# Queries and keys of three attention rows: one dense product each, spread to row groups through DRAM

## The chip, the cores and the metric

The kernel runs on one core of one Trainium2 chip. A core has five engines with their own instruction streams: PE (TensorE, matrix products), DVE (VectorE), ACT (ScalarE), POOL (GpSimd) and SP (SyncE), which here mostly issues DMAs. Each stream runs strictly in its order, and streams wait for each other through semaphores. In the profile, PEld is the loading of weights into PE, and PEq and SPq are the queues of PE and SP. The metric is the device time of one execution in microseconds. Three runs of the kernel before took 1353.03, 1360.2 and 1360.58 us, median 1360.2.

## The reference

Two layers, each of them attention plus a mixture of experts, both reading the same normalised input:

```
x  = [4, 512, 128]                         # 4 rows of 512 tokens, 128 features
xn = layernorm(x);  x = x + band_attention(xn) + gated_experts(xn)    # layer 0: 16 heads, window 64; 16 experts
xn = layernorm(x);  x = x + full_attention(xn) + relu_experts(xn)     # layer 1
```

What the change touches is the full attention of layer 1:

```
q, k, v = split(xn @ w_qkv)                # w_qkv [128, 384]; 16 heads of 8 features
attn    = softmax(q k^T / sqrt(128))       # per row and head, 512 x 512
out     = (attn v, heads side by side) @ w_out
```

All of it is in float32. The full attention is computed for every row, and the ReLU experts of a row need the same normalised row.

## The kernel before

Data is kept with features on the 128 partitions and tokens along the free dimension: `xT` holds the normalised rows of layer 1, 512 columns for each row. The kernel has two stages. In the first, which lasts to about 933 us, layer 0 is computed for the four rows, woven with the band attention of the row before (`band_values`) and with the first ReLU experts of layer 1 (`relu_experts`). In the second, from line 749 on, `full_attention` is woven with three things that are left over: the band values of the last row, the experts of row 2 and then the experts of row 3.

**The steps.** A head has 8 features, so four heads (a "group") are put into the four bands of 32 partitions of the PE array: head h of the group has partitions 32h to 32h+7. There are 4 rows with 4 groups each, so 16 groups, and in a group 4 blocks of 128 tokens, and in a block two pairs of heads. A pair of heads makes one score tile of 128 x 2 x 512 in PSUM. Each pair is computed twice: once ("m") keys by queries, where DVE takes the maximum over all keys (L952), and later ("x"), with that maximum worked into the product, where ACT takes the exponential (L959). The m pairs run twelve pairs ahead of the x pairs (`AHEAD`). One step of the loop normally has one m pair and one x pair, and with the first and last steps there are 128 steps. The four products of a step use four different bands of the array and are tied together by hand (`in_order`), and the first of a step waits until the maximum and the exponential of the step before have freed their PSUM tiles. With high priority, so ahead of all else, come the scores, the maxima, the exponentials and the weighting of values by a finished block (`weigh`, L852).

**Work between the scores.** Everything else is hung on steps by `at(t, ...)`: `queries` and `keys` a few steps ahead of a group's first m pair, `values` of a row, `with_maxima` after the last m pair of a group, `normalise` (two operations on DVE after a transposition), and at the end of a row `turned` and `project_out` (L882). They all take their PSUM tile from one buffer, `abank`. Between them stand the products of the ReLU experts (L388 in, L454 out), which are held to the pace of the steps by dependencies that only fix an order, and the band values: L321 transposes, L322 copies, L327 stores to DRAM (`by_s`), L339 loads back skewed (`wb`), L353 and L357 multiply. The framework's scheduler puts all instructions into one fixed order for each engine when the kernel is built.

**Queries and keys.** For the bands, the weights are spread out once with zeros: `wqk` has 32 columns for each head, of which 8 are filled. A group's queries are then one product of 128 x 128 by 128 x 512 (L823), of which only 4 x 8 of 128 output partitions hold anything, copied from PSUM by ACT (L827); the keys are another such product (L832), copied with a bias (L836) that puts a 1 into partition 32h+8, against which the negative maximum from the first pass is multiplied. So a row takes 8 such products, 4 groups by 2. `with_maxima` adds the transposed maxima to the queries (L843). `ex`, the exponentials of one block for four heads, has three buffers of 8 KB on each partition (`ep`).

**Other lines used later.** POOL sets up `wqk` (L765), the padded values `vaug` (L775, L776) and the maxima `nmax` (L777) at the start of the stage, and adds up the experts (L459). SP issues, in this order, what is ready: expert weights (L440, L442), routing rows (L444), band transfers (L312 `f`, L327, L339), and finished rows (L887).

Of the kernel before, what the change touches and what calls it, by code (L numbers as in the profile page):

```python
# [22 lines left out]
FP = mybir.dt.float32  # L23
# [5 lines left out]
P = 128  # L29
B, T, C = 4, 512, 128  # L30
# [67 lines left out]
def two_layers(ctx: ExitStack, tc: tile.TileContext, w: dict, consts: bass.AP, out: bass.AP):  # L98
    nc = tc.nc
# [5 lines left out]
    dram = ctx.enter_context(tc.tile_pool(name="dram", bufs=1, space=bass.MemoryType.DRAM))  # L105
# [19 lines left out]
    def c_(name):  # L125
        return cst[:, offs[name][0]:offs[name][1]]
# [160 lines left out]
    xT = keep.tile([C, B * T], FP, name="xT")  # L287
# [461 lines left out]
    ctx1 = ctx.enter_context(ExitStack())  # L749
    work = ctx1.enter_context(tc.tile_pool(name="work", bufs=2))  # L750
    one = ctx1.enter_context(tc.tile_pool(name="one", bufs=1))
    ep = ctx1.enter_context(tc.tile_pool(name="ep", bufs=3))
    ps_q = ctx1.enter_context(tc.tile_pool(name="ps_q", bufs=1, space=PSUM))
    ps_a = ctx1.enter_context(tc.tile_pool(name="ps_a", bufs=1, space=PSUM))

    def abank():
        return ps_a.tile([P, T], FP, tag="a", name="abank")

    w_qkv = one.tile([C, 3 * C], FP, name="w_qkv")
# [6 lines left out]
    for s in range(2):  # L766
        nc.vector.tensor_copy(
            wqk[:, s, :, :, 0:8].rearrange("c g h e -> c (g h) e"),
            w_qkv[:, s * C:(s + 1) * C].rearrange("c (h e) -> c h e", e=8),
        )  # L770

    vaug = [one.tile([P, TPB, H, 32], FP, name=f"vaug{i}") for i in range(2)]
    nmax = [one.tile([P, TPB, 4, 32], FP, name=f"nmax{i}") for i in range(2)]
# [8 lines left out]
    def full_attention():  # L782
# [6 lines left out]
        outs, q, k, qa, av, ex = {}, {}, {}, {}, {}, {}  # L789
# [18 lines left out]
        def values(b):  # L808
            pv = abank()
            for i in range(TPB):  # L810
                nc.tensor.matmul(  # L811
                    pv[:, i * P:(i + 1) * P], xT[:, b * T + i * P:b * T + (i + 1) * P],
                    w_qkv[:, 2 * C:3 * C], start=True, stop=True,
                )
            nc.vector.tensor_copy(
                vaug[b % 2][:, :, :, 0:8], pv.rearrange("p (t h e) -> p t h e", t=TPB, e=8)
            )
            outs[b] = work.tile([P, TPB, C], FP, tag="o1", name="o1")

        def queries(n):  # L820
            b, g = groups[n]
            pq = abank()
            nc.tensor.matmul(  # L823
                pq, wqk[:, 0, g].rearrange("c h e -> c (h e)"), xT[:, b * T:(b + 1) * T], start=True, stop=True
            )
            q[n] = work.tile([P, T], FP, tag="q", name="q")
            nc.scalar.copy(q[n], pq)  # L827
# [63 lines left out]
        def at(t, f, *args):  # L891
            todo.setdefault(t, []).append((f, args))
# [8 lines left out]
        for j in range(AHEAD, len(pairs)):  # L901
            x_step[j - AHEAD] = m_step[j] = len(steps)
            n, i, two = pairs[j - AHEAD]
# [4 lines left out]

        for n, (b, g) in enumerate(groups):
            t = m_step[8 * n]  # L910
            at(t - 5 if n > 1 else t - 3, queries, n)
            at(t - 3 if n > 1 else t - 2, keys, n)
            if g == 0:
                at(t + 1, values, b)
            at(m_step[8 * n + 7] + 1, with_maxima, n)
            for i in range(TPB):
                at(x_step[8 * n + 2 * i + 1] + 1, weigh, n, i)
            t = x_step[8 * n + 7]
            at(t + 3, normalise, n)
            if g == 3:  # L920
                at(t + 5, turned, b)
                at(t + 6, project_out, b)
# [43 lines left out]
    x_out = out.rearrange("b (t p) c -> p b t c", p=P)  # L966
    weave(
        (full_attention(), 106),
        (after(woven((band_values(B - 1, ready[B - 1][1]), 23), (experts[B - 2], 42)), relu_experts(B - 1)), 22 + 42 + 79 + 4),
    )  # L970
# [35 lines left out]
```

## Time and profile before

| | us |
|---|---|
| median of three runs | 1360.2 |
| the profiled execution, its own time | 1354.64 |
| its span, first to last instruction | 1352.8 |
| PE busy | 1165.9 |
| ACT busy | 1018.8 |
| DVE busy | 1007.9 |
| POOL busy | 87.3 |
| mean granted PE clock | 0.941 |

The busy times are of the whole execution and mix two stages with different limits; only the stage from about 933 us on has instructions of the lines that the diff touches. In the rows of groups of instructions, the first number is the time in which the engine was busy with the group, then the mean of one instruction in ns, then the idle time of the engine just ahead of them. PE appears with two records for each float32 product. In rows of the timeline the start and the length are in us, and the bracket at the end is the time in which the engine stood idle before, with the instruction that ended it.

### The profile page before, as it was taken

How to read it: one execution, taken by the hardware profiler on the slowest of the kernel's cores; microseconds unless marked ns; L12 is line 12 of the kernel's file. 1: busy time of each engine (PE TensorE's matmuls, PEld its weight loads, DVE VectorE, ACT ScalarE, POOL GpSimd, SP SyncE). 2: the span in 40 equal slices, each digit the busy share in tenths (PEclk: the TensorE clock that was granted, in tenths of full speed). 3: DMA queues.
4: the chain of work that ended last, by engine and by line, in shares of the span. 5: the costliest groups of instructions: out<-in, count | busy, mean ns of one | idle time of the engine just before them, and what ended most of it. 6: DMA issues, size and time to landing. Idle time of an engine off the chain costs nothing. (4 is left out here: it accounts for less than half of the span.)

```text
span 1352.8 us, 17415 instructions
## 1 busy us (share of the span) xinstructions
PE 1165.9 (86%) x6763; PEld 448.1 (33%) x6763; DVE 1007.9 (75%) x1085; ACT 1018.8 (75%) x1159; POOL 87.3 (6%) x68
## 2 busy tenths in 40 slices
PE   5676976677899879988987998897999999999997
PEld 2122322133434323334332343343333334333332
DVE  4999998999878899997779999843544445544441
ACT  4899997989888899999879999863454445555454
POOL 2000000000001021100100300002000000000000
PEclk9798988888999979998998999996999989999999
DMA  8121211446223434721244463223333210010100
GB/s 273 49 75 50 77 53 67 129 101 158 70 59 81 164 94 123 188 65 61 80 154 99 125 156 100 73 67 133 94 94 78 54 41 25 27 36 24 47 24 8
DMA packets 168524, 117.61 MB, mean 87 GB/s; under 512 B 66621, under 2 KB 149274, under 8 KB 166906
## 3 DMA queue, kind: packets, MB, share of 16 engines
q1 hardware_dynamic: 166970, 109.77, 29.6%
q0 software_dynamic: 1184, 6.29, 1.2%
q8 instruction: 54, 0.88, 0.3%
q10 hardware_dynamic: 288, 0.43, 0.1%
q14 instruction: 28, 0.23, 0.1%
HBM read 89.00 MB, written 27.46 MB: 86 GB/s over the span
## 5 line engine op out<-in xcount | busy, mean ns | idle before, releaser
L572 DVE TENSOR_TENSOR z<-proj 128x2044 f32<-128x2044 f32 (+31 forms) x256 | 553.6, 2185 | 22.6 <-PE lbank L586 13.5
L586 PE MATMUL lbank<-z,place 128*32 128x504 f32 (+18 forms) x2048 | 294.5, 649 | 105.3 <-ACT z L578 61.1
L952 DVE TENSOR_REDUCE nmax<-score 128x2 f32<-128x1024 f32 x128 | 156.3, 1225 | 194.1 <-PE score L935 193.7
L578 ACT ACTIVATE z<-z,posb 128x1024 f32<-128x1024 f32 (+31 forms) x256 | 266.7, 1097 | 8.1 <-DVE z L572 6.3
L574 ACT ACTIVATE z<-z,brep 128x2048 f32<-128x2048 f32 (+31 forms) x128 | 241.6, 1904 | 8.1 <-DVE z L572 7.0
L959 ACT ACTIVATE ex<-score 128x1024 f32<-128x1024 f32 x128 | 130.3, 1023 | 138.9 <-PE score L935 138.9
L935 PE MATMUL score<-k,q 32*128 32x512 f32 x512 | 142.6, 668 | 6.5 <-DVE nmax L952 4.0
L388 PE MATMUL bank<-xT,ew 128*128 128x512 f32 x256 | 137.0, 627 | 6.9 <-DVE e L628 5.7
L935 PE MATMUL score<-qa,k 32*128 32x512 f32 x512 | 139.5, 647 | 2.0 <-ACT ex L959 1.4
L459 POOL TENSOR_TENSOR total<-total,part 128x512 f32<-128x512 f32 x32 | 73.0, 2280 | 1044.1 <-DVE part L458 1018.2
L396 ACT ACTIVATE h<-bank,cols 128x512 f32<-128x512 f32 x144 | 97.8, 685 | 49.5 <-PE bank L388 48.9
L454 PE MATMUL bank<-h,ew 128*128 128x512 f32 x256 | 132.2, 614 | 2.5 <-ACT h L396 2.5
L586 PEld LDWEIGHTS lbank<-z,place 128*32 128x32 f32 x2048 | 44.3, 113 | 263.7 <-ACT z L578 128.7
L675 PEld LDWEIGHTS accbank<-wT,lin 128*128 128x128 f32 x512 | 71.3, 204 | 64.5 <-issue 38.3
L675 PE MATMUL accbank<-wT,lin 128*128 128x128 f32 x512 | 82.7, 300 | 9.0 <-DVE lin L673 8.9
L686 PE MATMUL gbank<-tT,wT 128*128 128x512 f32 x128 | 71.7, 642 | 19.1 <-DMA wT<-wT_all 18.3
L852 PE MATMUL accbank<-ex,vaug 128*32 128x512 f32 x512 | 70.6, 617 | 0.2 <-ACT ex L959 0.2
L693 PE MATMUL gbank<-tT,wT 128*128 128x512 f32 x128 | 67.4, 608 | 0.0
L689 ACT ACTIVATE glu<-gbank,gbt 128x512 f32<-128x512 f32 x64 | 43.8, 685 | 29.2 <-PE gbank L686 28.6
L454 PEld LDWEIGHTS bank<-h,ew 128*128 128x128 f32 x256 | 44.2, 193 | 59.6 <-issue 47.6
L935 PEld LDWEIGHTS score<-k,q 32*128 32x128 f32 x512 | 38.8, 190 | 75.2 <-ACT ex L959 31.3
L388 PEld LDWEIGHTS bank<-xT,ew 128*128 128x128 f32 x256 | 41.8, 193 | 66.2 <-issue 44.8
(188 smaller groups left out, 1192.3 us busy)
## 6 DMA issues: line engine op xcount, KB each, us to landing
r<-route SPq DMA_DIRECT2D x96, 256.0 KB, 3.4
ew<-in_L_ffn_W SPq DMA_DIRECT2D x64, 256.0 KB, 2.8
wb<-by_s SPq DMA_DIRECT2D x32, 512.0 KB, 5.5
wT<-wT_all SPq DMA_DIRECT2D x48, 192.0 KB, 2.4
by_t<-e SPq DMA_DIRECT2D x8, 1024.0 KB, 4.8
f<-by_t SPq DMA_DIRECT2D x128, 64.0 KB, 3.0
by_s<-g SPq DMA_DIRECT2D x16, 512.0 KB, 4.2
wb<-by_s SPq DMA_DIRECT2D x24, 256.0 KB, 3.0
```

The costliest lines, as they stand in the source:

```text
L388: mm = nc.tensor.matmul(ph, wt[:, c * P:(c + 1) * P], xT[:, b * T:(b + 1) * T], start=True, stop=True)
L396: nc.scalar.activation(h, ph, AF.Relu, bias=bias[:, c:c + 1])
L454: nc.tensor.matmul(py, old[1][:, c, :], old[0][c], start=(c == 0), stop=(c == 3))
L459: nc.gpsimd.tensor_tensor(total, total, part, ALU.add)
L572: nc.vector.tensor_tensor(z[:, :, :, 0:n], seen, own, ALU.subtract)
L574: nc.scalar.activation(z[:, :, :, 0:n], z[:, :, :, 0:n], AF.Gelu, bias=b_dmg)
L578: last = nc.scalar.activation(z[:, dq, :, 0:n], z[:, dq, :, 0:n], AF.Gelu, bias=posb[:, j:j + 1])
L586: mm = nc.tensor.matmul(ps[q:q + 32, t0:T], place[:, kind, 3 - dd:35 - dd], z[:, dq, hg, 0:n], start=(dd == 0), stop=(dd == 3),)
L675: nc.tensor.matmul(ya[:, i * P:(i + 1) * P], lin[:, i * P:(i + 1) * P], wT[:, 2, :], start=False, stop=(e == E0 - 1 and i == TPB - 1),)
L935: mm = nc.tensor.matmul(ps[:, h - two, :], own[r, i * P:(i + 1) * P], seen[r, :], start=True, stop=True)
L952: freed.append(nc.vector.tensor_reduce(nmax[n % 2][:, i, two:two + 2, 8:9], ps, AX.X, ALU.max, negate=True))
L959: freed.append(nc.scalar.activation(ex[n, i][:, two:two + 2, :], ps, AF.Exp, scale=inv))
```

## The change

For row 0 nothing changes. For rows 1 to 3, the four query projections of a row become one dense product with the 128 columns of `w_qkv` that belong to queries, and the four key projections one with those of the keys. A dense result has feature e of head (g, h) on partition 32g + 8h + e. ACT copies it from PSUM to `dense`, SP stores it to a DRAM tile `qk_d`, and four loads, one for each band h, bring the 8 features of four heads back to partitions 32h to 32h+7 of a tile that holds all four groups side by side, `qpad` or `kpad` (one pair for odd rows, one for even). The other partitions of these tiles are filled once, on POOL: zero in `qpad`, and in `kpad` the 0/1 column that the bias supplied until now. The four groups then use slices of these tiles. The dense products are hung 13 and 11 steps ahead of the row's first m pair. To make room for 32 KB of tiles and 4 KB of `dense` on each partition, `ex` has two buffers in place of three.

```diff
-    ep = ctx1.enter_context(tc.tile_pool(name="ep", bufs=3))
+    ep = ctx1.enter_context(tc.tile_pool(name="ep", bufs=2))
...
+    qpad = [one.tile([P, 4, T], FP, name=f"qpad{i}") for i in range(2)]
+    kpad = [one.tile([P, 4, T], FP, name=f"kpad{i}") for i in range(2)]
+    for i in range(2):
+        nc.gpsimd.memset(qpad[i], 0.0)
+        nc.gpsimd.tensor_copy(
+            kpad[i].rearrange("p g t -> p (g t)"), c_("ones8").to_broadcast([P, 4 * T])
+        )
+    qk_d = dram.tile([2, C, T], FP, name="qk_d")
...
+        def rows_apart(b, s):
+
+            pd = abank()
+            nc.tensor.matmul(
+                pd, w_qkv[:, s * C:(s + 1) * C], xT[:, b * T:(b + 1) * T], start=True, stop=True
+            )
+            dense = work.tile([P, T], FP, tag="dense", name="dense")
+            nc.scalar.copy(dense, pd)
+            nc.sync.dma_start(out=qk_d[s], in_=dense)
+            to = (qpad, kpad)[s][b % 2]
+            for h in range(4):
+                nc.sync.dma_start(
+                    out=to[32 * h:32 * h + 8], in_=qk_d[s].rearrange("(g h e) t -> h e g t", g=4, e=8)[h]
+                )
+            for g in range(4):
+                (q, k)[s][4 * b + g] = to[:, g, :]
...
         for n, (b, g) in enumerate(groups):
             t = m_step[8 * n]
-            at(t - 5 if n > 1 else t - 3, queries, n)
-            at(t - 3 if n > 1 else t - 2, keys, n)
+            if b == 0:
+                at(t - 5 if n > 1 else t - 3, queries, n)
+                at(t - 3 if n > 1 else t - 2, keys, n)
+            elif g == 0:
+                at(t - 13, rows_apart, b, 0)
+                at(t - 11, rows_apart, b, 1)
             if g == 0:
                 at(t + 1, values, b)
```

## The prediction

> **What bounds the kernel now.** I read the busy times by stretch first. The change touches nothing before the second layer's attention, which starts at 933 us, so only the last 420 us are in play.
>
> ```profile
> 0.00:915.00 915.00, 753.44 (x4409) 304.65 (x4409) 809.17 (x848) 807.82 (x902) 63.85 (x47) 0.93 0.37 103
> 935.00:985.00 50.00, 46.28 (x252) 17.12 (x248) 28.11 (x27) 18.92 (x25) 1.27 (x1) 0.89 0.31 76
> 1185.00:1235.00 50.00, 49.96 (x274) 15.91 (x270) 23.51 (x25) 26.23 (x31) 2.55 (x2) 1.00 0.13 37
> 1235.00:1285.00 50.00, 49.91 (x248) 16.46 (x245) 23.02 (x24) 24.86 (x30) 2.54 (x2) 1.00 0.11 33
> ```
>
> Columns after the stretch: PE, PEld, DVE, ACT, POOL busy, clock, DMA share, GB/s. PE is busy 99.9% of 1185 to 1285 with DVE and ACT at half. That alone says "take PE work away", but matmul ends are modelled, so I went to TensorE's timeline for what a step costs.
>
> ```profile
> 1002.74 0.70 PE L935 MATMUL score<-k,q 32*128 32x512 f32 x2
> ...
> 1003.81 1.07 PE L852 MATMUL accbank<-ex,vaug 128*32 128x512 f32 x8
> 1004.81 1.13 PE L823 MATMUL abank<-xT,wqk 128*128 128x512 f32 x2
> 1005.86 0.70 PE L935 MATMUL score<-k,q 32*128 32x512 f32 x2
> ...
> 1006.93 1.12 PE L388 MATMUL bank<-xT,ew 128*128 128x512 f32 x2
> 1007.90 1.02 PE L832 MATMUL abank<-xT,wqk 128*128 128x512 f32 x2
> 1008.85 0.70 PE L935 MATMUL score<-k,q 32*128 32x512 f32 x2
> ...
> 1009.92 1.06 PE L852 MATMUL accbank<-ex,vaug 128*32 128x512 f32 x8
> 1010.92 0.44 PE L235 MATMUL bank<-cst,avs 128*128 128x128 f32 x2
> 1011.40 0.70 PE L935 MATMUL score<-k,q 32*128 32x512 f32 x2
> ```
>
> Three steps, from first score product to first score product: 3.12 us (weighting plus one query projection), 2.99 (an expert product plus a key projection), 2.55 (weighting plus two transpositions; PE's own work is 1.03 + 1.06 + 0.2 = 2.3, the rest is waiting that the modelled ends hide). So a step has two limits. One is PE's own work: 1.03 us of scores, about 0.975 for each product of 128x128 by 512, 1.06 for a weighting, 0.1 for a transposition. The other is a floor of 2.55 us: scores 1.14, maximum on DVE 1.24 (the chain of waits alternates exactly these two), and hand-overs. A projection taken from a step near the floor gives about half of its time, in a floor step nothing.
>
> **What is removed.** Rows 1 to 3 lose 12 query and 12 key projections and gain 6 dense ones.
>
> ```profile
> L823 PE MATMUL abank<-xT,wqk 128*128 128x512 f32 x30 | 18.2, 693 | 0.0
> L832 PE MATMUL abank<-xT,wqk 128*128 128x512 f32 x30 | 16.1, 619 | 0.0
> ```
>
> Two records are one product, so 18 fewer at 0.975 is 17.6 us of PE time; ACT loses 12 x (0.586 + 0.687) = 15.3 us of copies and gains 6 x 0.586 = 3.5, but ACT is half idle.
>
> To see what of the 17.6 reaches the end I gave every step max(2.55, PE work), half steps 2.45, with small band products at 0.055 to 0.075. On the old order of TensorE this gives 376.6 us for 131 steps and half steps: 53 at the floor (134.6), 7 up to 2.8 (19.1), 60 around 3.05 (183.2), 11 longer (39.7). The timeline has 404.2 from first to last step, so 27.6 are stalls: 6.9 in the first five steps at half clock, 3.8 for a band reload (L353 waits for wb), 2.6 after it at half clock, 1.7 after the small router products, the rest waits of 0.3 to 1.5. On the order built for the changed kernel, same prices: 62 at the floor (157.8), 4 (10.7), 58 (176.3), 4 long (14.3), sum 359.1. The gain is 17.5. It exceeds what the same slots would give: taking the 24 out in place is worth only 12.7, and six new ones cost about 2.5, so 10. The other 7 come from a better spread: 11 long steps become 4. I take the built order, since TensorE runs strictly in it.
>
> **The fills on POOL.** Four tiles of 128x2048 are filled ahead of vaug and nmax. Behind them are vaug0, nmax0, vaug1, nmax1 and one sum (L459); the first maximum on DVE waits for nmax0, and all of DVE with it.
>
> ```profile
> 926.35 1.80 POOL L775 MEMSET vaug<- 128x2048 f32 x1
> 928.10 0.67 POOL L777 MEMSET nmax<- 128x512 f32 x1
> 931.14 1.26 POOL L459 TENSOR_TENSOR total<-total,part 128x512 f32<-128x512 f32 x1
> ...
> 935.33 2.36 DVE L952 TENSOR_REDUCE nmax<-score 128x2 f32<-128x1024 f32 x2 [7.03 <-PE score L935]
> ```
>
> nmax0 is ready at 928.8, needed at 935.3: 6.5 us of cover, all of which the fills use. Two memsets are 2 x 1.75 = 3.5. No POOL copy of this kind is in the trace. Below it is a memset (1.75), above it the two-input operation, 1.26 us for 512 columns, so 5.1 for 2048. The Trainium skill, GPSIMD Engine Reference (section 3.1, Elementwise), puts the two-input cost down to a read port shared by both inputs and gives one-input work about 1.03 cycles per element, an estimate of 1.8 us. The copy has one input, so I take 2.0: 3.5 + 4.0 = 7.5, a delay of 1.0. Ends: 0.5 late, or 13.7 and thus 7.2 late. PE is at half clock there anyway.
>
> **The way through DRAM.** Each row has two stores of 256 KB and eight loads of 64 KB on SP.
>
> ```profile
> 925.89 5.06 SPq L312 DMA_DIRECT2D f<-by_t  x8
> ...
> f<-by_t SPq DMA_DIRECT2D x32, 64.0 KB, 3.0
> out<-x SPq DMA_DIRECT2D x4, 256.0 KB, 2.3
> ```
>
> Issue is 0.63 us for a load of 64 KB, so SP gives 24 x 0.63 + 6 x 0.5 = 18 us in all. One side of a row takes a copy 0.6, store 2.3, three issues 1.9, last landing 3.0: 7.8 us. The Trainium skill speaks against this: DMA: Bandwidth & Descriptors (section Bandwidth, Measured) says to batch to 1 MiB and calls transfers under 64 KB, which these loads just reach, descriptor-dominated; with the fixed 2 us each of its section on the anatomy of one DMA, one after another, 24 loads would be 48 us and the kernel slower by 30. The row shows eight of them overlapping, and none is on PE's path: in the built order 31, 26 and 26 us of steps lie between the key product of rows 1, 2 and 3 and its first score. Cost 0; without cover 7.8 a side.
>
> What is queued on SP behind the query loads of row 1 is the band's by_s store, and behind the key store a band load, wb. The second band block has 11.3 us of steps from the key product to L353, of which by_s landing (4.2) and wb (4.8) with issues need about 8.9. So 2.5 us of slack take a delay of 1 to 2. Rows 2 and 3 have no band loads near. The third reload stall has one less filler before it: 0.5.
>
> ep falls from 3 buffers to 2: cost 0, since the weighting of a block stands on PE ahead of the scores whose exponential takes its buffer; if it did not, one exponential (1.02) would be late per block. The DVE addition with q reads a slice of the same shape, and kpad and qpad feed PE as k and q did: 0. Fewer users of the single abank could give back some of the 0.5 us waits at L823, an estimate of 0 to 2; I count none.
>
> Sum: -17.5 + 1.0 + 0.5 = -16. On the profiled execution, 1354.6 (span 1352.8 plus 1.8), that is 1338.6. That run lies 5.6 below the median of the runs, 1360.2 (1353.0 to 1360.6), whose changed counterpart is 1344.
>
> **Rivals.**
> 1. The floor eats more: the spread gains nothing. For: DVE waits on PE in nearly each step, so orders differ only by slots; small stalls of 0.3 to 1.5 show that packed steps meet late operands. Against: the model fits undisturbed steps within 0.1. Gain 10 - 1 = 9: 1351.
> 2. The fills run at the two-input rate: start 7.2 late, gain 17.5 - 7.7 = 10: 1350. For: POOL's sums took up to 9.8 us earlier. Against: that was with DVE busy, and DVE is idle here.
> 3. Slower: SP holds up the band at row 1. The expert weight load directly ahead of the query store waits for its buffer.
>
> ```profile
> SPq L440 <- PE bank L388: 124.4, 8, 22.3
> ```
>
> If it waits its longest, 22.3, with the query store and by_s behind it, 2.5 are covered, 19.8 go to L353, and 2.6 follow at half clock: -16 + 22.4 = +6, 1366. It beats the gain from a wait of 16 on. Against: the last product with that buffer stands just ahead of the dense query product.
>
> **Numbers.** Forecast 0.63, rivals 0.19, 0.11, 0.07. The range reaches from a gain of 24 (no fill delay, two or more stalls vanish) to 5: 1336 to 1355. About 1% is what a measurement of this kernel can tell from no change, so faster needs a gain of 13.6, only 2.4 below the forecast: 0.85 of the first case and little of the others, 0.57; slower 0.06.
>
> **What would show it.** The dense product six times and 18 fewer products; steps over 3.2 us reduced to a handful; nmax0 written near 936 and the first maximum about 1 us later after its scores; no PE wait named after qpad or kpad; the L353 wait near 4 us in the third reload and none at the second. Wrong if POOL's copies take over 4 us, if by_s of the second block waits for loads, or if new waits above 1 us fill the floor steps.

## The result and the profile after

The changed kernel takes 1340.88 us (median of 6 runs, 1337.61 to 1343.32), the kernel before on the same chips 1358.87 (6 runs): a ratio of 0.9868, 95% interval 0.9847 to 0.989. That is 18 us, where 16 were forecast and 1344 predicted.

The busy times by stretch, after (same columns as before: PE, PEld, DVE, ACT, POOL busy, clock, DMA share, GB/s):

```profile
0.00:915.00 915.00, 751.09 (x4386) 302.89 (x4387) 802.51 (x838) 804.92 (x899) 64.02 (x47) 0.93 0.37 103
941.00:991.00 50.00, 45.89 (x252) 17.59 (x252) 27.52 (x27) 19.54 (x27) 8.29 (x9) 0.90 0.40 99
1191.00:1241.00 50.00, 49.98 (x267) 15.97 (x260) 24.83 (x28) 24.27 (x28) 2.54 (x2) 1.00 0.18 45
1241.00:1291.00 50.00, 49.15 (x275) 15.94 (x273) 25.60 (x27) 24.89 (x29) 2.59 (x3) 1.00 0.13 38
```

PE looks as full as before; in these rows nothing shows that the stage became shorter. A product's record can hold waiting as well as work, since its end is modelled. Note also that in the first 915 us this execution got through fewer instructions (4386 on PE against 4409), although that code is the same. Its first score came at 941.7 us, not at 933.1. So the two spans, 1352.8 and 1341.3, differ by only 11.5 us. The lines of the score products give the stage itself, two before and two after (records; shortest, median and longest in ns; first and last start):

```profile
L935 PE MATMUL score<-k,q x512: 585/662/1218, 933.1 to 1318.8; 32*128 32x512 f32 x171
L935 PE MATMUL score<-qa,k x512: 587/692/1218, 958.0 to 1337.9; 32*128 32x512 f32 x171
...
L966 PE MATMUL score<-k,q x128: 587/692/1217, 941.7 to 1021.6; 32*128 32x512 f32 x128
L966 PE MATMUL score<-qa,kpad x384: 586/692/1217, 1056.9 to 1325.2; 32*128 32x512 f32 x192
```

From the first to the last score it took 404.8 us before and 383.5 after, 21.3 less. Over the profiled executions of this study the first score stood anywhere from 933.1 to 941.7. For a change in the second stage, first to last score is the cleaner measure, although each is one execution, and I use it below beside the medians.

TensorE's timeline, after, two steps of row 0, the first with a dense product for row 1:

```profile
981.10 0.70 PE L966 MATMUL score<-k,q 32*128 32x512 f32 x2
...
982.17 1.12 PE L388 MATMUL bank<-xT,ew 128*128 128x512 f32 x2
983.14 1.02 PE L833 MATMUL abank<-xT,w_qkv 128*128 128x512 f32 x2
984.09 0.70 PE L966 MATMUL score<-k,q 32*128 32x512 f32 x2
...
985.16 1.06 PE L879 MATMUL accbank<-ex,vaug 128*32 128x512 f32 x8
986.16 0.44 PE L321 MATMUL bank<-cst,f 128*128 128x128 f32 x2
986.64 0.70 PE L966 MATMUL score<-k,q 32*128 32x512 f32 x2
```

2.99 and 2.55 us: a dense product costs what a projection cost, and the floor is where it was. The groups of instructions on the products and copies (x12 records are six products):

```profile
L833 PE MATMUL abank<-xT,w_qkv 128*128 128x512 f32 x12 | 6.7, 636 | 0.0
L850 PE MATMUL abank<-xT,wqk 128*128 128x512 f32 x6 | 3.6, 678 | 0.0
L837 ACT COPY dense<-abank 128x512 f32<-128x512 f32 x6 | 3.5, 585 | 2.0 <-PE abank L833 2.0
```

The start of the stage on POOL, and the first maximum on DVE:

```profile
934.90 1.80 POOL L776 MEMSET qpad<- 128x2048 f32 x1
936.65 1.94 POOL L777 COPY kpad<-cst 128x2048 f32<-128x2048 f32 x1
938.54 1.80 POOL L776 MEMSET qpad<- 128x2048 f32 x1
940.29 1.89 POOL L777 COPY kpad<-cst 128x2048 f32<-128x2048 f32 x1
...
943.86 0.52 POOL L787 MEMSET nmax<- 128x512 f32 x1
```

```profile
944.41 2.36 DVE L983 TENSOR_REDUCE nmax<-score 128x2 f32<-128x1024 f32 x2 [7.55 <-POOL nmax L787]
```

The fills take 7.3 us from the first start to the last end, and the maximum now waits for nmax and not for its scores. But it starts 2.71 us after the first score (941.70), where it started 2.20 after before: 0.5 late. And the queue of SP on row 1:

```profile
984.81 0.33 SPq L838 DMA_DIRECT2D qk_d<-dense  x1
986.85 1.33 SPq L841 DMA_DIRECT2D qpad<-qk_d  x4
989.88 0.56 SPq L327 DMA_DIRECT2D by_s<-g  x1
993.21 0.35 SPq L838 DMA_DIRECT2D qk_d<-dense  x1
993.66 0.54 SPq L312 DMA_DIRECT2D f<-by_t  x1
994.25 0.60 SPq L339 DMA_DIRECT2D wb<-by_s  x1
995.30 1.31 SPq L841 DMA_DIRECT2D kpad<-qk_d  x4
```

Four loads are issued in 1.33 us, so 0.33 each, half of the 0.63 of f's loads, which have the same size but runs of 512 B where these have 2 KB. The band's by_s store stands right behind the query loads and is not held. The key loads are issued by 996.6, and the first score that reads kpad is at 1023.5.

### The profile page after: what moved, and what is told of

The parts are those of the page before. It is cut to its first block, busy times and chain, and to the rows that moved or that the text cites. A ratio compares the mean times of both kernels' runs of the same rounds, so it can differ in the third digit from the quotient of the medians.

```text
span 1341.3 us, 17381 instructions
## 1 busy us (share of the span) xinstructions
PE 1144.2 (85%) x6727; PEld 441.0 (33%) x6727; DVE 1008.7 (75%) x1085; ACT 1007.8 (75%) x1141; POOL 94.6 (7%) x72
## 5 line engine op out<-in xcount | busy, mean ns | idle before, releaser
L966 PE MATMUL score<-kpad,qpad 32*128 32x512 f32 x384 | 109.9, 645 | 4.1 <-DVE nmax L983 3.2
L966 PE MATMUL score<-qa,kpad 32*128 32x512 f32 x384 | 103.6, 648 | 2.2 <-ACT ex L990 2.2
L454 PEld LDWEIGHTS bank<-h,ew 128*128 128x128 f32 x256 | 44.1, 195 | 62.6 <-issue 50.6
L671 DVE SCALAR_TENSOR_TENSOR lin<-lin,r 128x512 f32<-128x512 f32 x64 | 45.7, 714 | 13.4 <-ACT lin L695 13.1
```

The source lines that it names most:

```text
L454: nc.tensor.matmul(py, old[1][:, c, :], old[0][c], start=(c == 0), stop=(c == 3))
L966: mm = nc.tensor.matmul(ps[:, h - two, :], own[r, i * P:(i + 1) * P], seen[r, :], start=True, stop=True)
```

## The experiments

All of them are edits of the changed kernel, except the one with two exponential buffers. The step sum is the working of the prediction, max(2.55, PE work) over the order in which each kernel's instructions were built.

| | step sum | first to last score | difference | median us | ratio to before |
|---|---|---|---|---|---|
| before | 376.6 | 404.8 | 28.2 | 1358.9 | 1 |
| before, two ex buffers | 376.6 | 402.3 | 25.7 | 1357.9 | 1.000 |
| changed | 359.1 | 383.5 | 24.4 | 1340.9 | 0.987 |
| products back | 383.0 | 406.7 | 23.7 | 1363.0 | 1.005 |
| copies back, in heaps | 359.0 | 392.3 | 33.3 | 1345.5 | 0.991 |
| copies back, spread | 359.1 | 383.3 | 24.2 | 1339.4 | 0.985 |
| no dense part at all | 354.9 | 380.2 | 25.3 | 1334.3 | 0.982 |
| dense, no DRAM | 359.1 | 381.2 | 22.1 | 1338.2 | 0.985 |
| queries only | 366.2 | 391.6 | 25.4 | 1345.5 | 0.992 |
| dense late | 367.0 | 411.1 | 44.1 | 1366.7 | 1.007 |
| fills twice | 360.0 | 390.7 | 30.7 | 1346.9 | 0.991 |
| fills last | 358.5 | 382.2 | 23.7 | 1339.2 | 0.985 |
| fills last, 17 ahead | 356.7 | 378.2 | 21.5 | 1331.5 | 0.980 |
| fills first, 17 ahead | 358.6 | 378.8 | 20.2 | 1332.9 | 0.983 |

Apart from three kernels in which something is made to wait (copies in heaps, dense late, fills twice), the difference lies between 20.2 and 28.2. It holds what the sum leaves out: the half clock at the start, the band reload, waits of 0.3 to 1.5. Two executions of one and the same order on TensorE (the first two rows) differ by 2.5, so what is below some 3 us is not read from a single row.

**Products back.**

```diff
+        def dead(n, s):
+            b, g = groups[n]
+            nc.tensor.matmul(
+                abank(), wqk[:, s, g].rearrange("c h e -> c (h e)"), xT[:, b * T:(b + 1) * T], start=True, stop=True
+            )
...
+            if b:
+                at(t - 5, dead, n, 0)
+                at(t - 3, dead, n, 1)
```

> The changed kernel, and with it the 24 old projections of rows 1 to 3 as products alone: same weights, same columns, at their old places, results unused, no copies. Theory (TensorE steps): each product is paid as in the step sum; on the order built for this kernel the sum is 383.0 us against 359.1 of the changed kernel and 376.6 of the one before, so 1340.9 + 23.9 = 1364.8, above the kernel before by about 6. Rival (the copies on ACT and the waits for them made the gain): products without copies bring back only what they hold up, under 8 us: 1341 to 1349.

1363.03 us, ratio 1.0047 (1.002 to 1.0074); first to last score 23.2 us more than the changed kernel, where the sum says 23.9. Nobody reads these products, and no copy comes back with them. So the time of the products on TensorE is enough for the whole gain, and with the six dense products on top the kernel is slower than before. The rival is out.

**Copies back**, first as they came, then tied to their steps.

```diff
+        def dead(n, s):
+            b, g = groups[n]
+            d = work.tile([P, T], FP, tag="dense", name="dead")
+            if s:
+                nc.scalar.activation(d, xT[:, b * T:(b + 1) * T], AF.Identity, bias=c_("ones8"))
+            else:
+                nc.scalar.copy(d, xT[:, b * T:(b + 1) * T])
...
+            if b:
+                at(t - 5, dead, n, 0)
+                at(t - 3, dead, n, 1)
```

> The changed kernel, and with it 24 copies on ACT of the old size (12 plain, 12 with a bias, 128x512) at the old places, from xT in SBUF, results unused, no products. Theory (TensorE steps): ACT is half idle in the stage, step sum 359.0, so 1341 within 3. Rival (copies): the 15.3 us of ACT work removed were the gain, and it goes again: 1353 to 1357.

1345.46, ratio 0.9908 (0.9893 to 0.9923): between the two forecasts. The timeline of ACT in this kernel shows why it decides nothing:

```profile
986.70 0.62 ACT L853 COPY dead<-xT 128x512 f32<-128x512 f32 x1
987.35 0.72 ACT L851 ACTIVATE dead<-xT,cst 128x512 f32<-128x512 f32 x1
988.11 0.62 ACT L853 COPY dead<-xT 128x512 f32<-128x512 f32 x1
988.76 0.72 ACT L851 ACTIVATE dead<-xT,cst 128x512 f32<-128x512 f32 x1
989.51 0.62 ACT L853 COPY dead<-xT 128x512 f32<-128x512 f32 x1
990.03 1.02 ACT L1001 ACTIVATE ex<-score 128x1024 f32<-128x1024 f32 x1
```

The copies depend on nothing but xT, so the scheduler put each row's eight in a heap, and one exponential stood behind it: three PE waits of 2.2 to 2.4 us, two of them with 3.4 us of half clock. In the kernel before, each copy waited for its own product. So the same with a tie:

```diff
+            tc.add_manual_dep(
+                i.ins, last[-1].ins.name,
+                mybir.DependencyInfo(mybir.DependencyClass.Sync, mybir.DependencyReason.DATA),
+                reason="spread over the steps",
+            )
```

> As the kernel with the 24 copies back, but each copy is tied to the step that it is hung on (it waits for the last product of that step), since without a tie they were built in three heaps of eight, and three exponentials came 2.2 us late behind each heap. Theory (copies stand beside the path): 1341 to 1343 and no PE wait for an exponential above 1 us. Rival (ACT's copies are part of the gain; the balance of the kernel with products back, 1.9 us above the one before from first to last score where the step sum says 6.4, leaves 4.5 for them): 1344 to 1347, in many small waits for exponentials.

1339.44, ratio 0.9854 (0.9831 to 0.9877). The waits of PE for exponentials are the same 2.2 us in three times as in the changed kernel, and first to last score is 383.3 against 383.5. So the 15.3 us of ACT work that the change removed were worth nothing that can be measured. The 4.5 us that I had set aside for them came from one profile each; by the medians the kernel with the products back is 5.3 us slower than the one before, where the sum says 6.4, so about 1 is left. One thing neither run brings back: a later product waiting for the copy that frees the single `abank`. The trace of before names only two PE waits for a copy of keys or queries from the first score on, 1.6 us together, and one of 0.8 is still there after the change.

**No dense part, and no DRAM.** The first loses the body of `rows_apart` but for the slices, the second only this (and both the tile `qk_d`). Both leave out part of the computation.

```diff
-            nc.sync.dma_start(out=qk_d[s], in_=dense)
...
-            for h in range(4):
-                nc.sync.dma_start(
-                    out=to[32 * h:32 * h + 8], in_=qk_d[s].rearrange("(g h e) t -> h e g t", g=4, e=8)[h]
-                )
```

> The changed kernel without the six dense products, their copies, stores and loads: rows 1 to 3 take their scores from the fills alone, so this part of the computation is left out. It shows what all that was added costs. Theory: step sum 354.9, 4.2 below the changed kernel: 1336.7. Rival (the way through DRAM holds up the band or PE): its waits go too, 8 us or more: below 1333.

> The changed kernel with the dense products and their copies, but without the stores and loads (the spread to the row groups is left out; scores of rows 1 to 3 come from the fills). It shows the DMAs alone. Theory: they are covered by 26 to 31 us of steps, step sum 359.1: 1341 within 3. Rival: the third band reload, which waited 4.5 us in the changed kernel against 3.5 before, is late because of them: 3 to 6 us faster, and the wait of L353 for wb falls.

1334.34 (ratio 0.9821, 0.9797 to 0.9845) and 1338.22 (0.9852, 0.9829 to 0.9875). From first to last score, 3.3 and 2.3 us less than the changed kernel. All that was added costs about what the sum says for six products, 4.2, and the 2.3 us for the 30 DMAs lie within the 2.5 by which one order differs from itself. With no DMA at all, the third band reload still waits 4.2 us for wb, against 4.5: SP's new queue is not its cause.

**Queries only.**

```diff
-            elif g == 0:
-                at(t - 13, rows_apart, b, 0)
-                at(t - 11, rows_apart, b, 1)
+            else:
+                if g == 0:
+                    at(t - 13, rows_apart, b, 0)
+                at(t - 3, keys, n)
```

> Only the queries of rows 1 to 3 are dense; the keys are projected by groups as before. Nine products fewer than before. Theory: step sum 366.2, 7.1 above the changed kernel: 1348. Rival (only the long steps counted, and they are gone with the first few products removed): most of the gain is already there, 1342 to 1344; or, if the gain needs both, it is near 1355.

1345.46, ratio 0.9919 (0.989 to 0.9949), 8.1 us more from first to last score than the changed kernel where the sum says 7.1. With nine of the eighteen products gone, 13.2 of the 21.3 us are there. By the medians it is only 4.6 us behind the changed kernel, where 7.1 were forecast.

**Dense late.**

```diff
-                at(t - 13, rows_apart, b, 0)
-                at(t - 11, rows_apart, b, 1)
+                at(t - 3, rows_apart, b, 0)
+                at(t - 2, rows_apart, b, 1)
```

> The dense products are hung 3 and 2 steps ahead of the row's first pair, not 13 and 11. Theory: the cover of the way through DRAM is then about 3 steps of 2.8 us against 7.8 needed, with the scheduler free to put the product a little elsewhere; the step sum of the built order is 367.0, and the three rows wait for kpad 1 to 5 us each, some with half clock after: 1341 + 8 + 3 to 18 = 1352 to 1367, with PE waits named after kpad. Rival (the loads land so fast that the lead does not matter): 1349, only the order's 8 us, and no wait for kpad.

1366.66, ratio 1.0069 (1.0048 to 1.009): slower than the kernel before, with the same work as the changed kernel. TensorE's timeline at the start of row 3 in this kernel:

```profile
1229.95 1.10 PE L833 MATMUL abank<-xT,w_qkv 128*128 128x512 f32 x2
...
1233.16 1.16 PE L821 MATMUL abank<-w_qkv,xT 128*128 128x128 f32 x8
1240.53 1.85 PE L966 MATMUL score<-kpad,qpad 32*128 32x512 f32 x2 [6.21 <-DMA kpad<-qk_d]
...
1243.17 1.64 PE L879 MATMUL accbank<-ex,vaug 128*32 128x512 f32 x8
```

PE has used up its other work by 1234.3 and stands for 6.2 us until the keys land; the clock is at half from 1237.6 to 1244.4, so for 3.9 us after the pause. From first to last score this adds 27.6 us: 8 in the order, the rest in waits for kpad (10.4 us in two PE waits) and for maxima, and in the slow clock after them. The way through DRAM costs nothing measurable in the changed kernel because of its place, not because it is short.

**Fills twice, fills last.** Twice: this loop stands in its place two times. Last: it is moved behind the loop that fills vaug and nmax.

```diff
+    for i in range(2):
+        nc.gpsimd.memset(qpad[i], 0.0)
+        nc.gpsimd.tensor_copy(
+            kpad[i].rearrange("p g t -> p (g t)"), c_("ones8").to_broadcast([P, 4 * T])
+        )
```

> The four fills on POOL are made twice, so 7.4 us more (1.75 and 1.93 each, twice) ahead of vaug and nmax. Theory: the cover is used up (the first maximum already waits about 0.5 us for nmax), so the first maximum comes 7.4 us later against its scores and the end 6 to 8 later: 1347 to 1349. Rival (the start is hidden by the half clock or made up by steps later): within 2 of 1341.

> The four fills on POOL stand behind vaug and nmax, where nothing waits for them before row 1; nothing else changed. Theory: the first maximum waits for its scores, no longer for nmax, and starts 0.5 us earlier after them; step sum 358.5 against 359.1: 1340, a gain of about 1 that is hardly measurable. Rival (PE is at half clock there, and the first full clock window decides): no difference, or one of 3.4 us either way.

Twice: 1346.87, ratio 0.9912 (0.9883 to 0.9942), so 6 us of the 7.4 put in arrive at the end. DVE's first two rows of the stage in that kernel:

```profile
948.21 0.69 DVE L830 COPY vaug<-abank 128x512 f32<-128x512 f32 x1 [14.26 <-POOL vaug L790]
948.81 2.35 DVE L988 TENSOR_REDUCE nmax<-score 128x2 f32<-128x1024 f32 x2
```

Its first score was at 938.6, so the maximum starts 10.2 us after it, 7.5 more than in the changed kernel: once the cover is gone, POOL's time is paid one for one. Last: 1339.21, ratio 0.9854 (0.9834 to 0.9875), not to be told from the changed kernel (the 0.5 us are less than its runs vary). DVE's first maximum waits for PE again there:

```profile
939.57 2.36 DVE L983 TENSOR_REDUCE nmax<-score 128x2 f32<-128x1024 f32 x2 [4.94 <-PE score L966]
```

**Two exponential buffers in the kernel before.**

```diff
-    ep = ctx1.enter_context(tc.tile_pool(name="ep", bufs=3))
+    ep = ctx1.enter_context(tc.tile_pool(name="ep", bufs=2))
```

> The kernel before with two buffers for the exponentials in place of three, nothing else. Theory: the weighting stands ahead of the scores that feed the next user of the buffer, so nothing: 1358.9 within 2, the same order on TensorE (sum 376.6). Rival: exponentials wait for weightings, up to 1 us in some blocks: 3 to 10 us slower.

1357.88, ratio 1.0 (0.9981 to 1.0019). Nothing.

**A better version.** With the fills last, the lead was varied on paper and the lowest step sum taken:

```diff
-                at(t - 13, rows_apart, b, 0)
-                at(t - 11, rows_apart, b, 1)
+                at(t - 17, rows_apart, b, 0)
+                at(t - 15, rows_apart, b, 1)
```

> The fills behind vaug and nmax, and the dense products hung 17 and 15 steps ahead of the row's first pair in place of 13 and 11. The step sum of the built order is 356.7, the lowest of the leads tried on paper, against 359.1 of the changed kernel. Theory: 1340.9 - 2.4 - 0.5 = 1338. Rival (stalls that the sum does not hold move with every order): anywhere from 1336 to 1344.

1331.52 us, ratio 0.9796 (0.9775 to 0.9817): it beats both kernels, and by more than the sum said (1338). Waits of PE from first to last score in the changed kernel, then in this one (in all, times, longest):

```profile
PE score L966 <- DVE nmax L983: 5.8, 13, 1.1
PE bank L353 <- DMA wb<-by_s: 5.4, 2, 4.5
PE score L966 <- ACT ex L990: 2.2, 3, 0.7
```

```profile
PE score L966 <- DVE nmax L983: 5.2, 14, 0.8
PE score L966 <- ACT ex L990: 2.2, 3, 0.7
PE abank L909 <- DVE qa L870: 2.0, 3, 0.7
```

The wait for wb is gone. In this order L353 of the last band block comes 11.5 us after the end of the last L321 (1077.49 after 1066.0), while copy, store and load between them take 9.8 where PE waits for them (1076.77 after 1066.98 in the changed kernel). The half clock that stood behind the wait is gone too. To see whether the lead alone does this, the same two lines were changed and the fills left where the change put them.

> The changed kernel with nothing but the lead altered: dense products 17 and 15 steps ahead, fills where the change put them. The step sum is 358.6 against 359.1. In the built order L353 of the last band block stands six steps behind the last L321, as against two in the changed kernel and four in the one with fills last and this lead. Theory: what made that version faster is the band reload, whose wait of 4.5 us and the slow step of 1.3 behind it go: 1340.9 - 0.5 - 5.8 = 1334.6, and no PE wait for wb above 1 us in that block. Rival (the version was faster through the sum and the start, the band wait being filled by other waits): 1339 to 1341.

1332.89 us, ratio 0.9832 (0.9806 to 0.9858), and one wait of 0.5 us for wb in place of 5.4 in two; from first to last score 4.7 us less than the changed kernel, of which the sum explains 0.5. So the lead alone is enough, and the place of the fills adds nothing to be measured. That it works through the room that its order happens to leave for the band reload fits the waits, but no run changed that room alone. In the medians the two kernels with this lead are 8.0 and 9.4 us ahead of the changed one, in the stage only 4.7 and 5.3; the rest lies outside the stage, where the code is the same, and stays open.

## Why the prediction was right

**The floor and the step sum.** The first to last score fell by 21.3 us; the sum on the built orders said 17.5. In the eleven kernels without an added wait, measurement less sum was 20.2 to 28.2 us, so the sum gives differences to within some 4 us of their mean while the sums themselves lie up to 28 apart. It also told "in place" (10) from "spread anew" (17.5): the first rival, 1351, is too slow by 10. The sum is the reason that the result was met. The 3.8 us between 21.3 and 17.5 are of the size of that scatter and are not explained one by one.

**ACT at nothing, ep at nothing.** Both measured as nothing within the scatter, by the copies spread over the steps and by two buffers in the kernel before.

**The fills.** 7.5 us were forecast, 7.3 measured; 1.0 late, measured 0.5. The copy with one input took 1.89 to 1.94 us, near the memset's 1.80 and near the estimate of 1.8 from the Trainium skill's GPSIMD Engine Reference (section 3.1, Elementwise), and far from the 5.1 that the two-input row would have made of it. The second rival falls with it. The cover of 6.5 us was real and is used up, as the doubled fills show.

**The way through DRAM at nothing.** No PE wait is named after qpad or kpad in the changed kernel. The leads of 26 to 31 us were far more than enough. The cost without cover was put at 7.8 a side, which was too low. In the late kernel 9.5 us pass from the end of row 3's last dense product (1231.05) to the score that waits for kpad (1240.53), and a half clock comes with it that I had left out of the price. SP issues the store at 1231.69 and the first key load at 1234.94, with three transfers for the experts between them. The rule on small transfers from the Trainium skill's DMA: Bandwidth & Descriptors (section Bandwidth, Measured) decides nothing here, and the page took it, like the fixed 2 us, on DMAs issued from GpSimd, while these are issued by SP. The issue of a load was overestimated: 0.33 us, not 0.63. The longer runs are the likely reason, but no run changed them alone.

**What was off in size.** The third band reload was to wait 0.5 longer and waited 1.0 longer (4.51 against 3.52), while the half clock behind it took 1.3 from the next step and not 2.6. "Steps over 3.2 reduced to a handful" was the sum's view without stalls: of the steps above 3.25 us on the timeline there were 26 before and 15 after. The third rival, SP holding up the band at row 1, did not come about: by_s was issued 1.7 us after the last query load.

**The profiled execution.** I had put it at 1338.6, and it was 1343.06: the stage gained 21.3 where 16 were forecast, but it began 8.6 us later, and what follows the last score took 1.2 more. That the forecast for the median (1344 against 1340.9) was nearer is in part luck: the offset of 5.6 us that I carried over from before lies within what the first stage alone varies, and the larger gain of the stage does not show in full in the medians.

## What to carry to other kernels

A busy share of 99.9% didn't say what a removed product is worth; the distance between two score products did. Write each step as the larger of its engine's own work and the floor of the chain that frees its buffers, sum it over the order that was built, and compare orders by that sum before trying them. A round trip through DRAM cost nothing measurable here with 26 to 31 us of other work between it and its first reader. Hung nine to ten steps later, the same instructions lost more than the whole change had gained, about 8 us of it through the order alone.

## What was not expected of the hardware

- The first 930 us of an execution varied by 8.6 us (first score from 933.1 to 941.7), half as much as the effect under study. DVE, ACT, POOL and SP have the same instructions in the same order up to about 927 us in all fourteen traces. A difference of two spans from one profile each would have shown 11.5 of 18 us.
- At the start of the stage TensorE stayed at half clock for 17 us before, from about 929 to 946, although it was busy for 14.7 of them with gaps of 0.4 to 0.8 us, and for 13.7 us in the changed kernel (busy for 11.1, gaps of 0.7 to 1.1). In the kernel with the fills last it was at full clock from the first score on: its first steps took 3.66 and 3.59 us in place of 4.61 and 4.54. There the pause ahead of the stage's first product was 1.3 us, against 2.6 before and 2.7 in the changed kernel; whether that decides it was not tested. Later on, 3.4 to 6.8 us of half clock came with each pause of 3.3 to 6.2 us, and 3.4 behind the run of small products (L418) in most of the traces.
